# The last ten steps of a message-passing layer in another order: a closer bound on finished nodes, other blocks behind the last sums

## The chip, the cores and the metric

The kernel runs on one core of a Trainium2 chip. The metric is device time in microseconds for one execution. TensorE is called PE here, VectorE DVE, ScalarE ACT, GpSimd POOL and SyncE SP.

## The reference, cut to what matters

One graph layer over 12,500 nodes with 128 features and 400,000 edges that are sorted by destination, then a residual and a layer norm:

```python
rbf = exp(-(distances[:, None] - centers) ** 2 / (2 * width * width))      # 50 centers
cut = 0.5 * (cos(pi * distances / CUTOFF) + 1) * (distances <= CUTOFF)
W = (silu(rbf @ fw1 + fb1) @ fw2 + fb2) * cut[:, None]
messages = (h[src] @ pw + pb) * W
agg = segment_sum(messages, dst, num_segments=12500)
h_new = h + (silu(agg @ mw1 + mb1) @ mw2 + mb2)
out = layernorm(h + h_new)                                                 # h = x
```

Edges longer than the cutoff give nothing. With these inputs 71,145 of the 400,000 are kept. Destinations are drawn as 12,500 u² with u uniform, so the number of edges at or below node n grows with the root of n, and the node that the first p edges have reached grows with p².

## The kernel before, in words

**Edges.** The kept edges are packed to the front in seven chunks, in order of destination, and then worked on in *quads* of 512 edges: 139 steps, `q` = 0 to `NL` - 1 = 138. A quad is two *pairs* of 256 edges, and each pair has a base, the first destination it touches. Quads of the last three chunks (from 69 on) are summed in two windows, one a pair; a window is at most 128 nodes wide. For each quad POOL gathers 512 rows of the projected features from DRAM with four indirect DMAs (L1016; eight quads have one part that SP copies row by row instead). PE and ACT make the radial weights (`basis`, `first`, `silu`, `second`), and DVE multiplies the two (`message`, L1094), builds a matrix that puts each edge on its node (`place`, L1106: the hot matrix), and PE sums with it (`sum_up`, L1126). DVE adds a window of sums to `aggT`, the table of all nodes in SBUF (`add`, L1160), at a base that a register holds (`base_of` one at a time, `bases_of` several). `added(q)` says how many quads' sums are in the table before step q: in pairs early on, one quad late, from NL - 14, without delay from NL - 4.

**Nodes.** Since destinations are sorted, a node is finished once the sums have passed it. `done_to(p)` bounds from below the node that pair p begins at: 0.162 (p - 4.9)². The bound is checked on the chip: `limits` (L344) makes it per pair, `unpack` compares it with the true bases, `count` (L1320) adds what failed, and a number over zero starts a repair behind the main program (`tc.If`, L1612). Node blocks of four tiles of 128 nodes (0 to 76), and at the end those of `TAIL` (80 and 84 with four tiles, 88 with two, 90 with one, 91 with two, 93 with three, 96 with the last two, the very last of 84 rows), go through these steps: `load_x`, `node_first` (PE with `mw1`, ACT's silu, L1169 and L1171), `node_second` (PE with `mw2`, L328), `node_stats` (DVE adds 2x and takes statistics, L1187 and L1191), `deviations` (DVE, and ACT's root, L1198 to L1202), `scales` (DVE, L1209), `normalize` (ACT, or DVE for tiles named in `on`; then a store, L171). Blocks 0 to 76 have their steps in `begin`, from `done_to`; those of the tail are written out by hand in `nodes`, `tail` and the lines behind the loop (L1515 to L1538).

**What sets the order.** The program is scheduled by hand: each engine does its instructions in the order written, and waits for what it needs. One step of the loop (L1451) issues `message`, then `nodes`, the gathers of later quads, `second` for two quads ahead, fillers on PE (`keep_busy`: matmuls whose result is not used), `sum_up`, the base registers, `place` for the next quad, `add`, `tail`. ACT must load a table when it goes from Silu to Square and Exp or to Sqrt and back; `activation(warm, half_pi, AF.Silu)` loads one ahead of need. PSUM has four banks that are handed out in turn, x tiles eight buffers.

In the kernel before, the last two steps and the end run like this: step NL - 2 sends message 137, block 90's second node step, block 88's statistics, block 84's normalization, PE's sums of 137, then the message of quad 138 in parts of one gather each as far as the third, the adds of 137 and block 91's first node step. Behind the loop come the last part and its sums, block 91's second step, the adds of 138, and then 90, 91, 93 and 96: five tiles (93 to 97) go through all node steps behind the last sums.

Of the kernel before, what the change touches and what calls it, by code (L numbers as in the profile page):

```python
# [15 lines left out]
OP = mybir.AluOpType  # L16
# [12 lines left out]
QT = 4  # L29
# [46 lines left out]
DONE = (0.162, 4.9)  # L76
TAIL = {80: 4, 84: 4, 88: 2, 90: 1, 91: 2, 93: 3, 96: 2}
# [4 lines left out]
def kernel(  # L82
# [59 lines left out]
    def load_x(t0, n=None):  # L142
        t = x4_sb[loaded[0] % X_BUFS]
        loaded[0] += 1
        node_dma(t0, t, x, False, n)
        x_sb[t0] = t
# [196 lines left out]

    def limits(v):  # L344
        for c in range(NC_):
            v.tensor_scalar(lim[:, c:c + 1], part_f[:64], float(2 * QB[c] - DONE[1]), 0.0,
                                    op0=OP.add, op1=OP.max)
        root = keep.tile([64, NC_], F32, name="root")
        v.tensor_scalar(root, lim, DONE[0], None, op0=OP.mult)
        v.tensor_mul(lim, root, lim)  # L350

    def done_to(p):
        return int(DONE[0] * max(p - DONE[1], 0) ** 2) - 1
# [798 lines left out]
    def added(q):  # L1152

        return max((q - 2) // 2 * 2 if q < NL - 14 else q - 1 if q < NL - 4 else q, 0)

    def add(q, ks=(0, 1)):
        pa = pa_of[q]
        for k in ks[:windows(q)]:
            to = aggT[:, ds(bases.pop((q, k)), wide(q))]
            nc.vector.tensor_add(to, to, pa[:, k * W:k * W + wide(q)])  # L1160

    zs_of, py_of, st_of = {}, {}, {}

    def node_first(t0):

        n = sum(rows(t0))
        pz = bank()
# [48 lines left out]
    def normalize(t0, rs, by, on=(), eng=nc.sync):  # L1216

        y = x_sb.pop(t0)
        for k, m in enumerate(rows(t0)):
            if k in on:  # L1220
                nc.vector.tensor_scalar(y[:m, k, :], y[:m, k, :], rs[:m, k:k + 1], by[:m, k:k + 1],
                                        op0=OP.mult, op1=OP.add)
            else:
                nc.scalar.activation(y[:m, k, :], y[:m, k, :], AF.Identity, bias=by[:m, k:k + 1],
                                     scale=rs[:m, k:k + 1])
        node_dma(t0, y, out, True, eng=eng)

# [29 lines left out]
    def nodes(q):  # L1257

        if deep:
            scales(*deep.pop())  # L1260
# [15 lines left out]
        for k, t0 in enumerate(TAIL):  # L1276
            if q == NL - 8 + k:
                load_x(t0)
        if q == NL - 5:
            st_of[0] = statistics()  # L1280
            node_stats(80, st_of[0])
        if q == NL - 3:
            node_stats(84, st_of[0][:, 4:])
            dev_of.append(deviations([84], st_of[0][:, 4:]))
            nc.scalar.activation(warm, half_pi, AF.Silu)
        if q == NL - 2:
            node_second(90)
            st_of[1] = statistics()
            node_stats(88, st_of[1])
            scales(*dev_of.pop(0))  # L1290
            normalize(*ready.pop(0))

    st_of, deep, dev_of = {}, [], []

    def tail(q):

        if q == NL - 7:
            node_first(80)
        if q == NL - 6:
            node_second(80)  # L1300
        if q == NL - 5:
            keep_busy(8)
            node_first(84)
        if q == NL - 4:
            node_second(84)
            node_first(88)
        if q == NL - 3:
            node_second(88)
            node_first(90)
        if q == NL - 2:  # L1310
            node_first(91)
# [8 lines left out]
    def count():  # L1320
# [8 lines left out]
        nc.vector.tensor_reduce(miss[:, 2:3], late_f, AX.X, OP.min)  # L1329
        nc.vector.tensor_scalar(miss[:, 2:3], miss[:, 2:3], 0.0, None, op0=OP.is_lt)  # L1330
        nc.vector.tensor_reduce(miss[:, 3:4], low, AX.X, OP.min)
        nc.vector.tensor_scalar(miss[:, 3:4], miss[:, 3:4], -2 * CUTOFF, None, op0=OP.is_lt)
        cp = bank()
        nc.tensor.matmul(cp[:1, :5], ones[:, 0:1], miss[:, :5], start=True, stop=True)
        nc.vector.tensor_reduce(miss[0:1, 0:1], cp[:1, :4], AX.X, OP.add)
        nc.vector.tensor_scalar(miss[0:1, 1:2], cp[:1, 4:5], float(-NL * QE), 0.0,
                                op0=OP.add, op1=OP.max)
        nc.vector.tensor_add(miss[0:1, 2:3], miss[0:1, 0:1], miss[0:1, 1:2])
# [112 lines left out]
    for q in range(NL - 1):  # L1451
# [29 lines left out]
        if at_once:  # L1481
            bases_of(list(now))
        else:
            for k in now:
                base_of(k, (0,))
        if q < NL - 2:
            place(q + 1)
        if q == NL - 4:
            place(NL - 1)
        if q == NL - 2:  # L1490
            for j in range(QT - 1):
                sum_up(NL - 1, message(NL - 1, (j, j + 1)), (j,))
        for k in now:
            if not at_once:
                base_of(k, (1,))
            if q == NL - 5 and k == now[0]:
                deep.append(deviations([80], st_of[0]))
                nc.scalar.activation(warm, half_pi, AF.Silu)
# [16 lines left out]
    q = NL - 1  # L1515
    base_of(q)
    sum_up(q, message(q, (QT - 1, QT)), (QT - 1,))
    node_second(91)
    add(q)
    node_stats(90, st_of[1][:, 2:])  # L1520
    for t0 in (93, 96):
        node_first(t0)
    node_stats(91, st_of[1][:, 3:])
    early_dev = deviations([88, 90, 91], st_of[1])
    assert not ready
    for t0 in (93, 96):
        node_second(t0)
    st = statistics()
    node_stats(93, st)
    scales(*early_dev)  # L1530
    for _ in (88, 90):
        normalize(*ready.pop(0))
    node_stats(96, st[:, 3:])
    last_dev = deviations([93, 96], st)
    normalize(*ready.pop(0), on=(0,))
# [111 lines left out]
```

## Time and profile before

| what | us |
|---|---|
| three runs, median (lowest, highest) | 726.54 (725.65, 727.59) |
| the profiled execution | 726.45 |
| its span, first to last instruction | 724.6 |
| busy in the span: PE, DVE, POOL, ACT | 586.3, 560.9, 532.7, 403.9 |
| first gather of the last quad starts | 700.59 |
| end of the last gather on POOL | 705.27 |
| last store issued | 719.76 |

The profile is of one execution. A row of its timeline gives the start from the span's first instruction, the duration, the engine, the line, the operation with output and inputs, and in brackets how long the engine had been idle and what ended it. PE's granted clock is given as a share of full speed; its mean is 0.912. DMA issue, register loads and branches are not counted as busy.

### The profile page before, as it was taken

To read this page: it belongs to the slowest core of one execution; us is meant where nothing else is said; L and a number is where in the kernel's file an instruction comes from. 1 tells how busy PE (TensorE), PEld (TensorE's weight loads), DVE (VectorE), ACT (ScalarE), POOL (GpSimd) and SP (SyncE) were. 2 spreads that over 40 slices of the span, in tenths; PEclk is the share of its full clock that TensorE was granted. 3 is DMA by queue.
4 is the path that set the end of the run, shared out by engine and by line. 5 is a ranking of instruction groups with operands and counts; after the bars stand their busy time and mean duration, and the time that the engine had idled before them with its cause. 6 is when DMAs were issued, how large, how long until landed. Compare 5 with 4: busy or idle time off the path is not lost.

```text
span 724.6 us, 13518 instructions
## 1 busy us (share of the span) xinstructions
PE 586.3 (81%) x3531; PEld 463.4 (64%) x3531; DVE 560.9 (77%) x1734; ACT 403.9 (56%) x573; POOL 532.7 (74%) x569
## 2 busy tenths in 40 slices
PE   6778868698889787598758896999896788797874
PEld 6666557676667566477536684877674566575753
DVE  8899799689999898699969794967556455564774
ACT  7547625364556566275444467557645744374683
POOL 6777777777777777777777777777777777777770
PEclk9998788899999899699988999899899988999996
DMA  8995442443334332433334344534443433345251
GB/s 278 324 314 182 146 125 75 112 115 96 100 90 127 98 94 74 147 93 89 98 102 113 100 125 121 158 98 138 115 112 98 141 98 109 102 122 149 57 154 56
DMA packets 53104, 91.38 MB, mean 126 GB/s; under 512 B 13824, under 2 KB 20576, under 8 KB 53018
## 3 DMA queue, kind: packets, MB, share of 16 engines
q1 hardware_dynamic: 34610, 53.34, 22.2%
q0 software_dynamic: 17840, 36.77, 20.5%
q8 instruction: 30, 0.49, 0.3%
q14 instruction: 56, 0.46, 0.2%
q10 hardware_dynamic: 568, 0.33, 0.2%
HBM read 74.59 MB, written 15.79 MB: 125 GB/s over the span
## 4 chain that ended last, share of the span: by engine, by line
DVE 29%; PE 19%; POOL 16%; DMA 14%; issue 14%; ACT 5%; DVEq 2%; SPq 1%; ACTq 0%; POOLq 0%
POOL quad L1016 14%; DMA quad<-proj,srci 8%; DVE hot L1106 6%; PE ph L1066 4%; PE bank L1083 4%; DVE msg L1094 3%; PE sums L1126 3%; PE bank L328 3%; POOL x L1016 2%; DVE aggT L1160 2%; DVE bank L492 2%; DVE nodes L496 2%; DVE r_d L486 2%; DMA x<-proj,srci 1%; DVEq L1135 1%
## 5 line engine op out<-in xcount | busy, mean ns | idle before, releaser
L1016 POOL DMA_INDIRECT quad<-proj,srci x405 | 384.5, 949 | 123.5 <-issue 98.8
L1083 PEld LDWEIGHTS bank<-fw_sb,s 128*128 128x128 f32 x1112 | 159.2, 206 | 61.5 <-issue 51.2
L1072 ACT ACTIVATE s<-ph 128x1024 f32<-128x1024 f32 x70 | 71.3, 1018 | 160.7 <-PE ph L1066 160.6
L1083 PE MATMUL bank<-fw_sb,s 128*128 128x128 f32 x1112 | 159.3, 290 | 0.0
L1066 PE MATMUL ph<-rbf,w_sb 102*128 102x512 f32 x278 | 138.8, 623 | 10.6 <-ACT s L1072 6.5
L1126 PEld LDWEIGHTS sums<-hot,msg 128*128 128x128 f32 x816 | 110.0, 201 | 50.1 <-issue 25.3
L1126 PE MATMUL sums<-hot,msg 128*128 128x80 f32 (+4 forms) x816 | 112.9, 284 | 10.5 <-DVE msg L1094 10.2
L1106 DVE TENSOR_SCALAR hot<-iota_n,dl,cut 128x80 f32<-128x80 f32 (+4 forms) x408 | 108.8, 339 | 14.7 <-PE sums L1126 12.9
L1016 POOL DMA_INDIRECT x<-proj,srci x95 | 90.8, 956 | 29.0 <-issue 24.1
L1080 PE MATMUL bank<-fb_b,ones_b 96*128 96x512 bf16 x139 | 56.1, 404 | 42.7 <-DVE msg L1094 15.6
L1094 DVE TENSOR_TENSOR msg<-bank,quad 128x512 f32<-128x512 f32 (+1 forms) x78 | 52.8, 677 | 43.0 <-DMA quad<-proj,srci 32.3
L1066 PEld LDWEIGHTS ph<-rbf,w_sb 102*128 102x128 f32 x278 | 49.2, 197 | 46.9 <-issue 35.2
L1160 DVE TENSOR_TENSOR aggT<-aggT,sums 128x80 f32 (+4 forms) x209 | 53.9, 258 | 28.0 <-PE sums L1126 11.9
L1057 ACT ACTIVATE rbf<-d,rbf_bias,rbf_scale 102x512 f32<-102x512 f32 x70 | 56.2, 803 | 33.3 <-DMA d<-near_d 33.3
L1016 POOL DMA_INDIRECT quad<-in_x_dram,srci x48 | 47.3, 985 | 15.4 <-issue 12.5
L328 PEld LDWEIGHTS bank<-pw_sb,xT 128*128 128x128 f32 (+1 forms) x292 | 41.6, 206 | 10.8 <-issue 5.5
L1094 DVE TENSOR_TENSOR quad<-bank,quad 128x512 f32<-128x512 f32 (+2 forms) x40 | 25.2, 633 | 28.2 <-DMA quad<-proj,srci 23.7
L1072 ACT ACT_TABLE_LOAD x36 | 46.2, 1283 | 0.6
L1126 PE MATMUL sums<-quad,quad 128*128 128x128 f32 (+3 forms) x296 | 44.9, 302 | 1.6 <-DVE quad L1094 1.5
L1058 ACT ACT_TABLE_LOAD x35 | 44.9, 1283 | 0.6
L1058 ACT ACTIVATE rbf<-rbf 102x512 f32<-102x512 f32 x70 | 44.1, 630 | 1.5
L1126 PEld LDWEIGHTS sums<-quad,quad 128*128 128x128 f32 x296 | 42.5, 220 | 2.4 <-DVE quad L1094 2.2
(268 smaller groups left out, 816.6 us busy)
## 6 DMA issues: line engine op xcount, KB each, us to landing
d<-near_d SPq DMA_DIRECT2D x70, 256.0 KB
dl<-proj SPq DMA_DIRECT2D x1024, 0.5 KB
x<-in_x_dram SPq DMA_DIRECT2D x46, 256.0 KB
quad<-proj,srci POOLq DMA_INDIRECT x405
proj<-hp SPq DMA_DIRECT2D x24, 256.0 KB
out_dram<-x SPq DMA_DIRECT2D x22, 256.0 KB
x<-proj,srci POOLq DMA_INDIRECT x95
r_d<-in_edge_weight_dram SPq DMA_DIRECT2D x5, 256.0 KB
```

The lines of the kernel that those rows point to most:

```text
L328: nc.tensor.matmul(to[:m, k, :], lT[:, k * P:k * P + m], w, start=False, stop=(k == a + c - 1))
L1016: nc.gpsimd.indirect_dma_start(out=got[:, j, :], out_offset=None, in_=proj if table is None else table, in_offset=bass.IndirectOffsetOnAxi ...
L1057: nc.scalar.activation(rbf[:u], d[:u], AF.Square, bias=rbf_bias[:u], scale=rbf_scale[:u])
L1058: nc.scalar.activation(rbf[:u], rbf[:u], AF.Exp, scale=-1.0 / (2.0 * width * width))
L1066: nc.tensor.matmul(ph[:, h, :], w1_sb[:2 * KR, h, :], rbf[:2 * KR], start=True, stop=True)
L1072: nc.scalar.activation(s[:, :n], ph[:, :n], AF.Silu)
L1080: nc.tensor.matmul(pu, ones_b[:, :P], bias_b["fb2"].rearrange("k j f -> k (j f)"), start=True, stop=False)
L1083: nc.tensor.matmul(pu[:, j * H:(j + 1) * H], s[:, j * P:(j + 1) * P], fw2_sb, start=False, stop=(j == QT - 1))
L1094: nc.vector.tensor_mul(msg[:, a:b, :], pu_of[q].rearrange("p (j f) -> p j f", j=QT)[:, a:b, :], got_of[q][:, a:b, :])
L1106: nc.vector.tensor_scalar(hot[:, j, :wide(q)], iota_n[:, :wide(q)], dl[:, at[0], at[1]], cut[:, at[0], at[1]], op0=OP.is_equal, op1=OP.mult)
L1126: nc.tensor.matmul(pa[:, k * W:k * W + wide(q)], msg[:, j, :], hot[:, j, :wide(q)], start=(j % n == 0), stop=(j % n == n - 1))
L1160: nc.vector.tensor_add(to, to, pa[:, k * W:k * W + wide(q)])
```

## The change

It reorders the steps from NL - 12 on and the lines behind the loop.

- **Bound.** `DONE` takes a smaller shift (2.0 for chunks 0 to 3, 1.3 for 4 to 6, instead of 4.9), and `LAST` raises it to four fixed nodes at pairs 268, 270, 274 and 276. The test in `limits` follows.
- **Branch.** A base under the bound no longer counts into the part of the repair that computes everything anew but into the one that goes over the nodes again, which now covers all blocks.
- **Blocks.** The tail is 80, 84 (four tiles), 88, 90, 92, 94, 96 (two each). Sums go in without delay from NL - 8 (before: NL - 4). Block 80 begins at NL - 9 (NL - 7), 84 at NL - 7 (NL - 5), 88 at NL - 6 (NL - 4), 90 at NL - 5 (NL - 3), 92 at NL - 3, and 94 and 96 behind the loop. The same formula gives blocks 40 and 52 to 76 a step earlier, 68 two.
- **Loads.** The tail's x tiles are loaded at NL - 12, - 11, - 10, - 9, - 5, - 5 and - 4 (before: one a step from NL - 8).
- **End.** The loop ends one step earlier; steps NL - 2 and NL - 1 are written out. Quad 138 goes in four parts, the first window added before the last part. Blocks 92 and 94 do their node steps between these parts; 96 is the only block whose first node step waits for the last sums. A Sqrt table load stands before the last two roots. The bases of quads 136 to 138 are loaded at once at NL - 3, and the hot matrix of 138 in that step (before: NL - 4).

The core of the diff:

```diff
-DONE = (0.162, 4.9)
-TAIL = {80: 4, 84: 4, 88: 2, 90: 1, 91: 2, 93: 3, 96: 2}
+DONE = (0.162, 2.0, 1.3)
+LAST = {268: 11520, 270: 11776, 274: 12032, 276: 12288}
+TAIL = {80: 4, 84: 4, 88: 2, 90: 2, 92: 2, 94: 2, 96: 2}
+LOAD_AT = {80: 12, 84: 11, 88: 10, 90: 9, 92: 5, 94: 5, 96: 4}
...
     def limits(v):
...
+        for p, n in LAST.items():
+            v.tensor_scalar(root[:, 0:1], part_f[:64], p - 2 * QB[-2] - 0.5, float(n),
+                            op0=OP.is_gt, op1=OP.mult)
+            v.tensor_tensor(lim[:, NC_ - 1:], lim[:, NC_ - 1:], root[:, 0:1], OP.max)
     def done_to(p):
-        return int(DONE[0] * max(p - DONE[1], 0) ** 2) - 1
+        s = shift_of(chunk_of(p // 2)) if p < 2 * NQ else 0
+        return max([int(DONE[0] * max(p - s, 0) ** 2) - 1] + [n for k, n in LAST.items() if p >= k])
...
-        return max((q - 2) // 2 * 2 if q < NL - 14 else q - 1 if q < NL - 4 else q, 0)
+        return max((q - 2) // 2 * 2 if q < NL - 14 else q - 1 if q < NL - 8 else q, 0)
...
     def nodes(q):
-        if deep:
-            scales(*deep.pop())
+        while deep:
+            scales(*deep.pop(0))
...
-        for k, t0 in enumerate(TAIL):
-            if q == NL - 8 + k:
+        for t0, k in LOAD_AT.items():
+            if q == NL - k:
                 load_x(t0)
...
+        for k, group, t0, at in ((6, [], 80, 0), (5, [80, 84], 84, 4), (4, [], 88, 0), (3, [88, 90], 90, 2)):
+            if q == NL - k:
+                if at == 0:
+                    st_of[1] = statistics()
+                node_stats(t0, st_of[1][:, at:])
+                if group:
+                    deep.append(deviations(group, st_of[1]))
+                    nc.scalar.activation(warm, half_pi, AF.Silu)
...
     def tail(q):
...
+        for k, t0, step in ((9, 80, node_first), (8, 80, node_second), (7, 84, node_first),
+                            (6, 84, node_second), (6, 88, node_first), (5, 88, node_second),
+                            (5, 90, node_first), (4, 90, node_second), (3, 92, node_first)):
+            if q == NL - k:
+                step(t0)
+        if NL - 6 < q < NL - 2:
+            keep_busy(4)
...
-    for q in range(NL - 1):
+    for q in range(NL - 2):
...
+        elif q == NL - 3:
+            bases_of([q, q + 1, q + 2])
...
+        for k in {NL - 4: (q + 1, q + 2), NL - 3: (q + 2,)}.get(q, (q + 1,)):
+            place(k)
...
+    p, q = NL - 2, NL - 1
+    msg = message(p)
+    scales(*deep.pop(0))
+    while ready:
+        normalize(*ready.pop(0))
+    node_second(92)
+    keep_busy(6)
+    sum_up(p, msg)
+    st = statistics()
+    node_stats(92, st)
+    sum_up(q, message(q, (0, 1)), (0,))
+    dev = deviations([92], st)
+    nc.scalar.activation(warm, half_pi, AF.Silu)
+    sum_up(q, message(q, (1, 2)), (1,))
+    add(p)
+    node_first(94)
+    scales(*dev)
+    sum_up(q, message(q, (2, 3)), (2,))
+    add(q, (0,))
+    keep_busy(2)
+    for _ in range(len(ready)):
+        normalize(*ready.pop(0))
+    sum_up(q, message(q, (3, 4)), (3,))
+    node_second(94)
+    add(q, (1,))
+    node_first(96)
+    nc.scalar.activation(warm, half_pi, AF.Sqrt)
+    node_stats(94, st[:, 2:])
+    keep_busy(2)
+    node_second(96)
+    devs = [deviations([94], st[:, 2:])]
+    node_stats(96, st[:, 4:])
+    devs.append(deviations([96], st[:, 4:]))
+    for dev in devs:
+        scales(*dev)
...
+    for t0, k in ((94, 0), (96, 0), (96, 1), (94, 1)):
+        scaled(*ys[t0], k, (t0, k) in ((96, 0), (94, 1)))
+    for a, eng in ((0, nc.sync), (1, nc.scalar)):
+        m = rows(96)[a]
+        eng.dma_start(out[(96 + a) * P:(96 + a) * P + m], ys[96][1][:m, a])
+    node_dma(94, ys[94][1], out, True)
```

`scaled` is the normalization of one tile, taken out of `normalize`. The lines that these replace (L1276 to L1291, L1297 to L1311, L1486 to L1498, L1515 to L1538) are in the listing above.

106 lines of the change are left out of this document (29 added, 77 removed).

## The prediction

> **What bounds the kernel now.** I read the page, then the windows by stage, then the timeline of the last 50 us. Times are us from the span's start. Steps are named by their quad, 0 to 138: NL-7 is step 132, NL-1 is 138. "Block 92" is the block of node tiles that begins at tile 92.
>
> ```profile
> L1016 POOL DMA_INDIRECT quad<-proj,srci x405 | 384.5, 949 | 123.5 <-issue 98.8
> ...
> L1072 ACT ACTIVATE s<-ph 128x1024 f32<-128x1024 f32 x70 | 71.3, 1018 | 160.7 <-PE ph L1066 160.6
> ```
> ```profile
> 600.00:640.00 40.00, 32.84 (x176) 25.06 (x176) 22.89 (x78) 19.17 (x25) 30.23 (x33) 0.87 0.36 105
> ...
> 690.00:700.00 10.00, 7.69 (x37) 5.20 (x36) 7.18 (x27) 8.40 (x18) 7.56 (x9) 0.83 0.49 151
> ...
> 706.00:710.00 4.00, 4.00 (x19) 3.79 (x18) 1.24 (x5) 1.04 (x3) 0.00 (x0) 0.57 0.23 82
> ...
> 718.50:724.60 6.10, 0.00 (x0) 0.00 (x0) 0.00 (x0) 0.00 (x0) 0.00 (x0) 0.50 0.24 76
> ```
>
> The columns of the windows are busy us (and instructions) of PE, PEld, DVE, ACT and POOL, then PE's granted clock; those of the timeline below are start, duration, engine, line, operation, and the idle time before it. In the first fence a gather costs POOL 0.95 us, and the idle time before the gathers (123.5 us over 405) is mostly issue, 0.25 us each. The row 600:640 has 33 gathers in 40 us: about 1.25 us for one, 5.0 us for a quad of four, and nothing between. PE and DVE are far from full there (32.8 and 22.9 of 40 us). **POOL's gathers set the pace**, and the change leaves their number and order alone. So only what follows the last gather can give time, and what the new order puts late before it can cost some.
>
> ```profile
> 678.26 0.69 DVE L1094 TENSOR_TENSOR msg<-bank,quad 128x512 f32<-128x512 f32 x1 [0.72 <-DMA quad<-proj,srci]
> ...
> 684.35 1.05 PE L1126 MATMUL sums<-hot,msg 128*128 128x128 f32 x8
> ...
> 688.11 3.19 ACT L1224 ACTIVATE x<-x,by,rs 128x128 f32<-128x128 f32 x8 [0.73 <-DVE by L1210]
> ...
> 692.76 2.08 PE L1169 MATMUL bank<-aggT,mw_sb 128*128 128x512 f32 x2 [1.90 <-DVE aggT L1160]
> ...
> 693.22 0.17 DVE L1209 RECIPROCAL rs<-dev 128x4 f32<-128x4 f32 x1
> 693.42 0.16 DVE L1210 SCALAR_TENSOR_TENSOR by<-both_m,rs 128x4 f32<-128x4 f32 x1
> ...
> 699.62 0.38 ACT L1171 ACTIVATE zs<-bank 128x256 f32<-128x256 f32 x1 [1.09 <-PE bank L1169]
> ...
> 701.94 1.11 DVE L1106 TENSOR_SCALAR hot<-iota_n,dl,cut 128x128 f32<-128x128 f32 x4 [0.26 <-issue]
> 702.18 1.28 ACT L1202 ACT_TABLE_LOAD   x1
> ...
> 703.47 0.30 ACT L1202 ACTIVATE dev<-v,eps 128x4 f32<-128x4 f32 x1
> 703.49 0.68 DVE L1094 TENSOR_TENSOR msg<-bank,quad 128x512 f32<-128x512 f32 x1
> ...
> 704.20 0.36 DVE L1187 SCALAR_TENSOR_TENSOR x<-x,bank 128x256 f32<-128x256 f32 x1
> 704.33 0.94 POOL L1016 DMA_INDIRECT quad<-proj,srci  x1 [0.30 <-issue]
> 704.59 0.49 DVE L1191 BATCH_NORM_STATS2 st<-x 128x6 f32<-128x128 f32 x2
> ...
> 705.08 0.20 ACT L1285 ACTIVATE warm<-half_pi 128x1 f32<-128x1 f32 x1
> ...
> 705.39 1.65 ACT L1224 ACTIVATE x<-x,by,rs 128x128 f32<-128x128 f32 x4
> 705.50 0.22 PE L325 MATMUL bank<-mb_b,ones_b 96*128 96x128 bf16 x1 [1.38 <-ACT zs L1171]
> ```
> ```profile
> 706.26 1.86 PE L1126 MATMUL sums<-hot,msg 128*128 128x128 f32 x8
> 706.61 0.29 DVE L1094 TENSOR_TENSOR quad<-bank,quad 128x128 f32<-128x128 f32 x1 [0.53 <-DMA quad<-proj,srci]
> ...
> 708.16 0.61 DVE L1160 TENSOR_TENSOR aggT<-aggT,sums 128x128 f32 x2 [1.26 <-PE sums L1126]
> ...
> 709.27 0.29 DVE L1094 TENSOR_TENSOR quad<-bank,quad 128x128 f32<-128x128 f32 x1 [0.50 <-issue]
> ...
> 710.01 0.39 PE L1126 MATMUL sums<-quad,quad 128*128 128x128 f32 x2
> ...
> 710.43 0.61 DVE L1160 TENSOR_TENSOR aggT<-aggT,sums 128x128 f32 x2 [0.86 <-PE sums L1126]
> ...
> 712.16 0.54 PE L1169 MATMUL bank<-aggT,mw_sb 128*128 128x212 f32 x2
> ...
> 712.44 0.17 DVE L1198 TENSOR_TENSOR dif<-st 128x5 f32<-128x5 f32 x1
> ...
> 712.84 0.17 DVE L1201 TENSOR_TENSOR v<-both_m,dif 128x5 f32<-128x5 f32 x1
> ...
> 714.03 0.40 PE L328 MATMUL bank<-mw_sb,zs 128*84 128x128 f32 x2
> ...
> 715.34 0.48 DVE L1187 SCALAR_TENSOR_TENSOR x<-x,bank 128x128 f32<-128x128 f32 x2
> ...
> 715.74 0.47 DVE L1191 BATCH_NORM_STATS2 st<-x 128x6 f32<-128x128 f32 x2
> ...
> 716.74 0.34 DVE L1221 TENSOR_SCALAR x<-x,rs,by 128x128 f32<-128x128 f32 x1
> ...
> 718.50 1.26 ACTq L171 DMA_DIRECT2D out_dram<-x  x2
> ```
>
> The last gather starts at 704.33 and ends at 705.27; the span ends 19.3 us later. The third part of quad 138 (its gather started 703.08, one period of 1.25 before the last) was waited for until 706.61, about 3.5 us after its start, so the last part is there by some 707.8 at the latest. Its message, however, starts at 709.27: DVE stood at 708.16 for PE's sums of quad 137, and PE stood at 705.50 for ACT, which had done a load of the Sqrt table, one of the Silu table (702.18 to 705.28) and block 90's silu. So 1.5 us lie between the data and the message. Then come 10.5 us to the last store's issue (718.50 + 1.26 = 719.76) with five tiles in them (93 to 97), and 4.84 us (719.76 to 724.6) in which no engine computes: stores land, programs end.
>
> **The change part by part.**
>
> *The bound and its test.* `limits` gets eight more instructions on a 64x1 column, chained in pairs, and `count` one.
>
> ```profile
> 74.54 0.16 DVE L350 TENSOR_TENSOR lim<-root,lim 64x7 f32<-64x7 f32 x1
> 75.82 0.41 DVE L936 SCALAR_TENSOR_TENSOR dl<-dl 10x256 f32<-10x256 f32 x1 [1.12 <-ACT dl L927]
> ```
>
> The nearest row is the product at 74.54: 0.16 us, 0.19 if each waits for the one before, so at most 1.5 us. DVE idles 1.12 us right behind, for ACT, and that covers them but for 0.4 us; POOL's queue was filled before. I take 0, keep 0 to 0.4, and see no way to a gain. The bound must hold for these inputs, or the repair at the end runs. Counted in the inputs: 71,145 edges are kept, room is 71,168; the pair with least room is pair 27 (destination 107, bound 101.25), and of the four fixed ones pair 270 (11,790 against 11,776). It holds everywhere.
>
> *Early blocks.* With the closer bound, blocks 40 and 52 to 76 begin one step earlier (68 two), and 80 begins at NL-9 instead of NL-7.
>
> ```profile
> 653.93 0.69 DVE L1094 TENSOR_TENSOR quad<-bank,quad 128x512 f32<-128x512 f32 x1 [3.11 <-DMA quad<-proj,srci]
> ```
>
> DVE has such waits for the gather (3.11 us here) in these steps; they hide one more pair of adds or 0.87 us of statistics. Cost 0, while a step's work stays under 5.0 us; without that cover, the work itself.
>
> *Steps 132 to 137*, counted forward from message 132 with the rows' durations, each engine in its program's order. A step's DVE work: message 0.6, statistics 1.6 for four tiles or 0.8 for two (704.20 to 705.0), deviations 0.6 (712.44 to 713.01), scales 0.4, hot matrix 1.1, both adds 0.55; for base registers, which leave no busy row, I take 0.3 (above 0, and at most the 0.50 us of issue ahead of the message at 709.27, in which quad 138's are loaded). Message 132 at 678.26, then 4.75 us of work: message 133 at 683.0. It comes in two parts: 5.1 us with scales and four-tile statistics, message 134 at 688.0. Another 4.7: message 135 at 692.7. These are the gathers' own times within a us.
>
> ACT is the tight queue: a block of four tiles costs it 3.2 us to normalize (688.11), a Sqrt 1.28 + 0.3, the Silu after it 1.28 + 0.2. Step 132's Sqrt waits for DVE until 681.1; Silu load to 682.7, silu of quads 136 and 137 to 683.7, block 84's to 684.8 (its sums come 1.1 us behind the adds at 683.1), blocks 64 and 68 to 688.0, silu of quad 138 and of block 88 to 689.4, blocks 72 and 76 to 692.6, Sqrt to 694.2, Silu to 695.7, block 90 to 696.1, blocks 80 and 84 to 699.3, Sqrt to 700.9, Silu to 702.4. So in step 135 DVE waits at `scales` until 694.2, 0.9 us behind its message, and behind it stand block 88's statistics, two hot matrices and the adds (0.8 + 0.4 + 2.2 + 0.3 + 0.55): message 136 at 698.4, step 136 (0.6 + 0.8 + 0.6 + 0.4 + 1.1 + 0.55) to 702.5. **Message 137 at 702.5** instead of 703.49, where its gathers have just landed.
>
> PE per step: the adds' wait, node work, two matmul groups of 1.1 and 0.9 (684.35: eight matmuls), the fillers: 3.7 to 4.7 us at full clock, under 5.0.
>
> *The loads of x* move up: 80 to 90 to steps 127 to 130, where their buffers' last stores are two steps old; 92 and 94 stand on SP's queue behind the stores of 72 and 76 (692.6), 96 behind those of 80 and 84 (699.3). Block 92 is needed at 704.3, 96 at 711: cost 0 unless ACT slips some 8 us.
>
> *The end.* After message 137: scales, block 92's statistics behind PE's node step (704.3 to 705.1), part 0 of quad 138. PE: node step to 704.3, six fillers to 705.6, sums 137 to 706.5. ACT: blocks 88 and 90 in 1.65 to 705.3, Sqrt load and deviation to 706.9, Silu to 708.4, block 94's silu to 708.8. DVE: adds 137 to 707.1, then scales of 92 (ACT at 706.9) to 707.5, part 2 there, add of the first window, **last part at 708.2** instead of 709.27: gain 1.1. It is still not the gather's time, because two messages stand behind `scales`.
>
> From there: message and sums 1.2 (709.27 to 710.40), to 709.4; PE's second step for block 94 to 709.9; first step for 96, whose add is done, 0.6 with its bias: 710.5; silu 0.4: 711.0; second step 0.8, two tiles like the one at 714.03: 711.8; two sums with x and two statistics 0.87: 712.7; deviations 0.6: 713.3; ACT's root 0.3 with the table loaded beforehand; two scales 0.8 beside and behind it: 714.1; a normalization of a tile each on ACT (1.65 for four) and DVE, two deep: 714.6; issue 0.6: 715.2 on ACT, about the same on SP. That is 7.0 us where 10.5 were, gain 3.5. SP's last store is now 128 KB and its queue ends as late as ACT's, for which I take back 0.3. **Sum: 1.1 + 3.5 - 0.3 = 4.3 us.** The profiled execution took 726.45 us, of which 1.85 lie around the span; its time is 0.09 under the median of 726.54. So 726.45 - 4.3 = 722.2 us.
>
> *A rule against it.* PE's clock fell after short gaps: 1.90 us at 692.76, whose pair took 2.08 us (the window has 0.83), 1.38 us at 705.50 (0.57; eight matmuls in 1.86 instead of 1.05). The new order has one such gap in step 132, while PE waits for the adds behind block 76's statistics (sums done near 680.8, adds from 682.6: 1.8 us), and only shorter ones behind the fillers. The Trainium skill, "TensorE: Matmul & The Clock Gate", Part 1, drops the clock only after an idle window of about 3.4 us; by it no gap here would lower the clock and the sum would stand. The rows disagree, so the drop is a rival.
>
> **The rivals.**
>
> *ACT ends late* (chance 0.20): each 1 us that ACT's chain lies behind my count moves `scales` in step 135 and all behind it, since message 137 has no slack left. For it: nine table loads in its queue and little idle; against it: every term is a row. Two us late gives 724.2.
>
> *Half clock at the end* (0.08): the PE pieces between 708.5 and 711.8 are 2.9 us at full clock; doubled, as at 706.26, they take 2.9 more: 725.1.
>
> *Half clock from step 132 on* (0.09), the other side: the adds of a step now wait for that step's sums from NL-8 on, and node steps wait for the adds, so PE and DVE run in one loop. At full clock a round is under 4.7 us; at half clock PE's 3.5 us become 7 and the round 7.5 to 8. From 5.0 us on the loop, not the gathers, sets the pace: 2.5 us or more in each of three or four steps, 8 to 10 us, against the 4.3 gained: 730. For it: the gap in step 132 and the window of 0.57; against it: fillers in steps 134 to 137, and the clock came back within 10 us each time.
>
> *The bound fails and the repair runs* (0.01): some 27 blocks one after another, each of several us: over 800. The count of the inputs speaks against it.
>
> *Table loads with a drain* (0.01): the deviation at 703.47 starts 0.01 us behind the end of its 1.28 us load. If a switch held ACT as long again as its load, nine of them from step 132 on would add 11.5 us: 733. A hold of that kind is the rule of the Trainium skill, "ScalarE: Activation LUTs", What ACT_TABLE_LOAD costs (2.66 us for every switch, load and drain); the row at 703.47 contradicts it.
>
> **How the numbers follow.** The forecast, 722.2, has 0.61; its own range is 720.6 (last part at 707.0, soon after it lands, and 0.4 less behind it) to 723.8. With ACT's 724.2 to 724.6 and the clock's 725.1 the range to 725.5 holds eight in ten. 0.3% is 2.2 us, about what a measurement of this kernel can tell from no change: faster by more, below 724.4, is the forecast and half of ACT's rival, 0.71; within, the other half and the short clock drop, 0.18; slower, the loop and the two small ones, 0.11.
>
> **What would show it.** The last gather again at 704 within 0.5 us (else the pace moved). Message 137 near 702.5; `scales` of step 135 waiting for ACT about 1 us; the last part's message near 708.2; from it to the last store's issue 7 us; one silu and one root behind the last sums. Wrong if PE's clock in 700 to 712 is under 0.8, if ACT's silu of block 94 comes after 710, or if messages 134 to 136 come over 1 us later than in the quoted rows.

## The result, and the profile after

The changed kernel took 1006.75 us (median of 6 runs, 1005.79 to 1007.4), the one before 725.96 beside it: a ratio of 1.3866 (1.3846 to 1.3885). The forecast was 722.2. Three rows of the page of the changed kernel, whose span is 1005.5 us, say where to look: POOL's busy tenths in 40 slices, PE's clock in the same slices, and the group of the gathers (count, busy us and mean ns, idle us before them).

```profile
POOL 6777777777777777777777777777210000000000
...
PEclk9998778999889997997999989999866666655655
...
L1027 POOL DMA_INDIRECT quad<-proj,srci x413 | 392.3, 950 | 149.2 <-issue 98.2
```

A slice is 25 us. The program's own gathers end in slice 29, at 706.7 us, about where they ended before (705.27); slice 30 still has four gathers, and then follow ten slices without POOL, at a PE clock of 5 to 6 tenths. And there are 413 gathers, where 405 were: two quads of four more than the program's 139 steps need. That is code which stands in a branch behind the main program. Of the same page, the chain that ended last, by engine and by line:

```profile
ACT 12%; DVE 6%; PE 5%; issue 2%; DMA 0%; ACTq 0%; DVEq 0%
PE bank L331 5%; ACT x L1243 4%; ACT L1184 3%; DVE st L1204 2%; ACT L1215 2%; DVE x L1200 2%; ACT zs L1184 2%; ACT dev L1215 1%; DVE rs L1222 1%; DVE by L1223 0%; DVE v L1214 0%; DVE dif L1211 0%; DVE dif L1213 0%; DMA quad<-proj,srci 0%; PE sums L1137 0%
```

Nearly all of it is node work. The timeline shows one block of it:

```profile
770.40 1.65 ACT L1243 ACTIVATE x<-x,by,rs 128x128 f32<-128x128 f32 x4 [0.44 <-DVE by L1223]
772.06 1.28 ACT L1184 ACT_TABLE_LOAD   x1
...
773.35 0.60 ACT L1184 ACTIVATE zs<-bank 128x512 f32<-128x512 f32 x1
774.00 2.08 PE L331 MATMUL bank<-mw_sb,zs 128*128 128x128 f32 x8 [5.38 <-ACT zs L1184]
...
778.38 1.28 ACT L1215 ACT_TABLE_LOAD   x1 [4.43 <-DVE v L1214]
779.68 0.30 ACT L1215 ACTIVATE dev<-v,eps 128x4 f32<-128x4 f32 x1
...
780.42 1.65 ACT L1243 ACTIVATE x<-x,by,rs 128x128 f32<-128x128 f32 x4 [0.44 <-DVE by L1223]
```

One block of four tiles from 770.40 to 780.42, 10.0 us, each engine waiting for the one ahead of it, with two table loads on the way. **The repair ran**, the part of it that goes over the nodes again, now over all 27 blocks.

*Which pair fails.* Chunk 0 is read as 128 rows of edges, and the first 32 kept edges of each row go to quads 0 to 7. So the rest of chunk 0, up to quad 13, is not the sorted list's continuation: it goes over the rows again, from the first one on, with what remained of each. Quad 13 has base 91. The new bound for its two pairs, 26 and 27, which the test of chunk 1 covers with the shift of 2.0, is 93.31 and 101.25; the old one was 72 and 79. No node block begins that early, so the alarm saves nothing.

The main program ends in front of the repair, and its windows can be held against those of before (columns as in the prediction):

```profile
600.00:640.00 40.00, 31.06 (x179) 23.06 (x178) 22.30 (x74) 22.27 (x33) 30.24 (x33) 0.96 0.40 113
690.00:700.00 10.00, 7.45 (x49) 6.00 (x48) 8.44 (x33) 8.72 (x20) 7.56 (x9) 0.93 0.54 162
706.00:710.00 4.00, 2.38 (x16) 1.48 (x15) 2.56 (x10) 3.94 (x8) 3.09 (x4) 1.00 0.22 61
```

33 gathers in 40 us again, so the pace is the same. In 706 to 710 PE now has its full clock (0.57 before), but it computes for 2.38 us of 4; ACT is full. The rows of step 135 show most of the reason, in the order of time:

```profile
694.86 0.69 DVE L1105 TENSOR_TENSOR quad<-bank,quad 128x512 f32<-128x512 f32 x1
694.87 1.28 ACT L1215 ACT_TABLE_LOAD   x1
...
696.49 1.28 ACT L1304 ACT_TABLE_LOAD   x1
696.50 0.20 DVE L1222 RECIPROCAL rs<-dev 128x8 f32<-128x8 f32 x1 [0.94 <-ACT dev L1215]
...
697.89 0.36 ACT L1184 ACTIVATE zs<-bank 128x256 f32<-128x256 f32 x1
...
698.30 0.38 PE L1091 MATMUL bank<-fb_b,ones_b 96*128 96x512 bf16 x1 [1.74 <-ACT zs L1184]
698.52 1.83 PE L1094 MATMUL bank<-fw_sb,s 128*128 128x128 f32 x8
...
700.99 1.55 PE L1137 MATMUL sums<-quad,quad 128*128 128x128 f32 x8
...
702.58 0.61 DVE L1171 TENSOR_TENSOR aggT<-aggT,sums 128x128 f32 x2 [2.71 <-PE sums L1137]
...
703.53 0.69 DVE L1105 TENSOR_TENSOR msg<-bank,quad 128x512 f32<-128x512 f32 x1 [0.34 <-DVE aggT L1171]
```

PE's `second` for quad 137 stands 1.74 us for ACT's silu of block 90 (697.89). It needs none of its data; the bank that is handed out next is the one this silu still has to read, and the silu stands behind two table loads. Then the eight matmuls take 1.83 us (1.06 at full clock), the sums come at 700.99, DVE waits 2.71 us for them, and message 136 starts at 703.53 instead of the forecast 698.4. Not all of these 5.1 us come from step 135: message 132, which waited for its gather, was 1.3 us late (679.54), and message 135 was 2.2 us late (694.86, forecast 692.7). Step 135 itself took 8.67 us from message to message, forecast 5.7, and so added 3.0.

```profile
705.72 0.95 POOL L1027 DMA_INDIRECT quad<-proj,srci  x1 [0.30 <-issue]
...
706.44 1.11 DVE L1117 TENSOR_SCALAR quad<-iota_n,dl,cut 128x128 f32<-128x128 f32 x4 [0.78 <-issue]
...
714.34 0.28 DVE L1105 TENSOR_TENSOR quad<-bank,quad 128x128 f32<-128x128 f32 x1
...
720.54 0.37 SPq L174 DMA_DIRECT2D out_dram<-x  x1
```

The last gather of quad 138 starts at 705.72 (those behind it are the repair's), 1.4 us later than before and outside the 704 within 0.5 that the forecast named as its sign; the base registers take 0.78 us of issue at 706.44. The last part's message is at 714.34, and the last store's issue ends at 720.91 (720.54 + 0.37). So two questions went to the chip: what the repair costs, and why the main program, which ought to have ended 4.3 us sooner, did not.

### The profile page after: what moved, and what is told of

The parts are those of the page before. It is cut to its first block, busy times and chain, and to the rows that moved or that the text cites. A ratio compares the mean times of both kernels' runs of the same rounds, so it can differ in the third digit from the quotient of the medians.

```text
span 1005.5 us, 14992 instructions
## 1 busy us (share of the span) xinstructions
PE 707.7 (70%) x3886; PEld 533.1 (53%) x3886; DVE 631.0 (63%) x2076; ACT 546.5 (54%) x794; POOL 540.6 (54%) x577
## 5 line engine op out<-in xcount | busy, mean ns | idle before, releaser
L1027 POOL DMA_INDIRECT quad<-proj,srci x413 | 392.3, 950 | 149.2 <-issue 98.2
L331 PE MATMUL bank<-mw_sb,zs 128*128 128x128 f32 x392 | 78.4, 359 | 143.7 <-ACT zs L1184 143.7
L1094 PE MATMUL bank<-fw_sb,s 128*128 128x128 f32 x1128 | 164.5, 293 | 0.5 <-ACT s L1083 0.5
L1083 ACT ACTIVATE s<-ph 128x1024 f32<-128x1024 f32 (+1 forms) x72 | 72.4, 1005 | 169.0 <-PE ph L1077 168.9
L331 PEld LDWEIGHTS bank<-mw_sb,zs 128*128 128x128 f32 x392 | 69.4, 259 | 173.1 <-ACT zs L1184 172.0
L1077 PE MATMUL ph<-rbf,w_sb 102*128 102x512 f32 x282 | 147.0, 646 | 18.6 <-ACT rbf L1069 16.1
L1200 DVE SCALAR_TENSOR_TENSOR x<-x,bank 128x512 f32<-128x512 f32 (+3 forms) x56 | 33.9, 609 | 143.8 <-PE bank L331 143.8
L1243 ACT ACTIVATE x<-x,by,rs 128x128 f32<-128x128 f32 x194 | 79.6, 482 | 14.3 <-DVE by L1223 14.3
L1182 PE MATMUL bank<-aggT,mw_sb 128*128 128x512 f32 (+2 forms) x108 | 71.1, 750 | 5.5 <-DVE aggT L1171 5.3
L1184 ACT ACTIVATE zs<-bank 128x512 f32<-128x512 f32 (+2 forms) x54 | 30.0, 555 | 42.6 <-PE bank L1182 42.2
```

The source lines that it names most:

```text
L331: nc.tensor.matmul(to[:m, k, :], lT[:, k * P:k * P + m], w, start=False, stop=(k == a + c - 1))
L1027: nc.gpsimd.indirect_dma_start(out=got[:, j, :], out_offset=None, in_=proj if table is None else table, in_offset=bass.IndirectOffsetOnAxi ...
L1077: nc.tensor.matmul(ph[:, h, :], w1_sb[:2 * KR, h, :], rbf[:2 * KR], start=True, stop=True)
L1083: nc.scalar.activation(s[:, :n], ph[:, :n], AF.Silu)
L1094: nc.tensor.matmul(pu[:, j * H:(j + 1) * H], s[:, j * P:(j + 1) * P], fw2_sb, start=False, stop=(j == QT - 1))
L1182: nc.tensor.matmul(pz[:, :n], mw1_sb, aggT[:, t0 * P:t0 * P + n], start=False, stop=True)
```

## The experiments

The first four ran on one chip (before: 727.28 us there).

**bound_ok.** The closer bound everywhere but in chunk 1's test:

```diff
-            v.tensor_scalar(lim[:, c:c + 1], part_f[:64], float(2 * QB[c] - shift_of(c)), 0.0,
+            v.tensor_scalar(lim[:, c:c + 1], part_f[:64], float(2 * QB[c] - (4.9 if c == 1 else shift_of(c))), 0.0,
```

> The changed kernel with one edit: the tested bound of chunk 1 has the old shift of 4.9. Theory A: the repair ran only because the first pairs of chunk 1 (26 and 27, base 91) lie under their new bounds of 93.3 and 101.3; then 405 gathers instead of 413, no repair, and by the trace of the changed kernel the main path ends with the last store's issue at 720.9, so the span ends near 725.7 and the time is near 727.5, no gain over the kernel before. Rival 1: another pair fails too, the repair stays and so do 1006 us. Rival 2: the main path in that trace is slowed by the repair's own gathers, and the recorded sum of 722.2 stands.

731.05 us, ratio 1.0045 (1.0031 to 1.0058). So chunk 1's pairs alone set off the repair, and it costs 1006.75 - 731.05 = 276 us. And the new order is slower than the old even without it. The 727.5 of theory A was too low by 3.5: in this profile the last gather starts 2.1 us later than in the changed kernel's, and the end behind the last store's issue takes 6.6 us instead of 4.84.

**few_blocks.** The changed kernel, with fewer blocks in the repair that runs:

```diff
             for q in range(NL, NQ):
                 more(q)
-            finish(blocks)
+            finish(list(TAIL))
```

> The changed kernel with its bound as it is, and a repair that goes over the 7 blocks of the tail instead of all 27 (the other nodes keep the main path's values). If the repair's cost is its blocks one by one, 10.0 us each as the rows between 760 and 800 show, it takes 20 of 10.0 less: about 806. If it were the two extra quads and their code, over 950.

808.05 us, in one run: 198.7 us less for 20 blocks, 9.9 each, as the 10.0 us between the rows at 770.40 and 780.42 say.

**bank_turn.** bound_ok, and in three steps `second` takes the bank behind the next one:

```diff
         s = s_of.pop(q)
+        if NL - 4 <= q < NL - 1:
+            free.append(free.pop(0))
         pu = bank()
```

> bound_ok, and second of quads 135, 136 and 137 takes the next PSUM bank in turn instead of the first, which block 90's (or 84's, 88's) first node step has just given back. Theory B: the main path lost its gain because PE stood 1.74 us for that bank until ACT's silu, behind two table loads, and the slow clock that followed: second of 137 starts right behind the fillers, message 136 comes 2 to 3 us earlier, the time is 2 to 4 us under bound_ok. Theory C: ACT's queue as a whole is late; then the same time as bound_ok within 1 us.

728.52 us, ratio 1.0019 (1.0003 to 1.0035), 2.5 under bound_ok. Its timeline:

```profile
696.02 0.38 PE L1093 MATMUL bank<-fb_b,ones_b 96*128 96x512 bf16 x1
...
697.56 1.05 PE L1139 MATMUL sums<-quad,quad 128*128 128x128 f32 x8
...
699.39 0.60 DVE L1173 TENSOR_TENSOR aggT<-aggT,sums 128x128 f32 x2
...
700.28 0.69 DVE L1107 TENSOR_TENSOR msg<-bank,quad 128x512 f32<-128x512 f32 x1 [0.28 <-DVE aggT L1173]
...
711.17 0.28 DVE L1107 TENSOR_TENSOR quad<-bank,quad 128x128 f32<-128x128 f32 x1
...
717.37 0.37 SPq L174 DMA_DIRECT2D out_dram<-x  x1
```

`second` no longer waits, the sums take 1.05 us instead of 1.55, DVE's adds follow without a wait, and message 136 is at 700.28. From message 135 (694.48) to it are 5.8 us, as forecast (5.7).

**root_later.** bound_ok, with the deviations of blocks 80 and 84 and the Silu load behind that step's node work instead of ahead of it:

```diff
-                if group:
+                if group and k != 5:
...
+        if q == NL - 5:
+            deep.append(deviations([80, 84], st_of[1]))
+            nc.scalar.activation(warm, half_pi, AF.Silu)
         if NL - 6 < q < NL - 2:
             keep_busy(4)
```

> bound_ok, and in step 134 the deviations of blocks 80 and 84 with their two table loads stand behind block 90's first node step, so its silu comes ahead of the loads. Theory B: second of 137 starts some 1.5 us earlier, but DVE waits up to 1 us longer at the scales of step 135: 0 to 2 us under bound_ok, less than bank_turn. Theory C: slower than bound_ok or the same.

731.16 us, ratio 1.0053 (1.0040 to 1.0067): no gain. But the wait for the bank is gone here too, and the profile shows where the gain went:

```profile
698.20 0.38 PE L1091 MATMUL bank<-fb_b,ones_b 96*128 96x512 bf16 x1
...
703.76 0.69 DVE L1105 TENSOR_TENSOR msg<-bank,quad 128x512 f32<-128x512 f32 x1 [0.29 <-DVE aggT L1171]
...
708.35 0.85 PE L1182 MATMUL bank<-aggT,mw_sb 128*128 128x256 f32 x2 [2.58 <-DVE aggT L1171]
...
709.00 1.91 PE L1325 MATMUL ph<-mb_b,ones_b 96*128 96x512 bf16 x4
...
712.02 0.42 DVE L1200 SCALAR_TENSOR_TENSOR x<-x,bank 128x256 f32<-128x256 f32 x1 [2.73 <-PE bank L331]
```

`second` starts at 698.20 without a wait, and message 136 comes 3.8 us ahead of the last gather's start, where it came 2.3 ahead in bound_ok: 1.5 us won, as theory B said. Then, in step 136, PE waits 2.58 us for the adds and goes on at half clock (0.56 granted from 708.3 to 712; four fillers take 1.91 us instead of 1.03), and DVE waits 2.73 us for it. So the silu behind the two table loads did hold the bank, and this run's unchanged time doesn't clear the loads.

**turn_short, before_long, sums_first, early_alone.** These four ran on another chip; their edits stand with the second runs below.

> The kernel of bank_turn, with the repair of nodes (which does not run) written for the seven blocks of the tail, as in the kernel before, instead of for all 27: less code behind the main program, nothing else. Theory A (the 6.7 us from the last store's issue to the span's end, against 4.84 before, hold a wait of SP for its instructions, and where it falls depends on how much code is jumped over): the end is back near 4.9 us, and the time falls from 728.5 to 726.7. Theory B (the end is longer because SP's last store is now 128 KB, or for another reason that lies in the order of the main program): the end stays at 6.6 to 6.8 us, and the time at 728.5.

> The kernel before, with the repair of nodes (which does not run) written for all 27 blocks as in the changed kernel: more code behind the main program, nothing else. Theory A (the end's length comes from the code that is jumped over): the end goes from 4.84 us to about 6.7, and the time from 727.3 to 729.1. Theory B (it comes from the new order's last stores): the end stays at 4.8 to 4.9 and the time at 727.3.

> turn_short, with two more edits in the last steps: no fillers before the sums of quad 137 (in bank_turn's trace six of them held PE from 706.9 to 708.4 while the message had been there since 705.5), and in step 136 the adds stand ahead of the hot matrix of 138 (there DVE began the adds at 704.29, 1.8 us after PE had ended the sums). Theory A (behind the last gather DVE and PE wait for one another, and each of the two stands on that chain): the last part's message comes some 1.9 us sooner behind the last gather (5.67 us in bank_turn, 3.8 here), and the time is 1.9 us under turn_short's: 724.8 if that one is at 726.7. Theory B (without the fillers PE's clock falls and the pieces behind the last sums take double): the last part's message comes sooner, but from it to the last issue it is 8 to 9 us instead of 6.6, and the time is that of turn_short.

> The kernel before with the closer bound alone (with the old one for chunk 1, as in bound_ok), so that blocks 40 and 52 to 76 begin a step earlier and the test of the bound is the longer one; the tail, its order and the end stay as before. Theory A (the earlier blocks and the test cost nothing, and the last gather's start varies from run to run by a us): 727.3, within 0.7 us. Theory B (bank_turn's last gather began 1.2 us later than before, and bound_ok's 3.5 us later, because of the earlier blocks or the test): 728.5 or more, with the last gather 1 us or more later than 704.3.

On that chip all took 1,098 to 1,102 us, the kernel before too (1097.66), with ratios 1.0011, 0.9966, 1.0015 and 0.9974, whose intervals all hold 1. They tell nothing of 2 us. All four were run again, on a third chip.

**turn_short_again.** bank_turn, with the repair, which does not run, as long as before the change (`-finish(blocks)`, `+finish(list(TAIL))`).

> The kernel of turn_short again, because on the chip of its first run every kernel, the one before too, took some 1,098 us, with waits for issue all over, which hides 2 us. Theory A (the end is longer in bank_turn because SP waits for its instructions, and that hangs on the code that is jumped over): from the last store's issue to the span's end about 4.9 us instead of 6.76, and a ratio to the kernel before near 0.9995 instead of 1.0019. Theory B (the end is longer for a reason in the main program's order): 6.6 to 6.8 us and 1.0019.

726.54 us, ratio 1.0002 (0.9986 to 1.0017). SP's instructions at the program's last line (count, ns, first and last start) in the kernel before, in bank_turn and in turn_short_again:

```profile
L1643 SPq EVENT_SEMAPHORE  x14: 17/28/28, 722.9 to 724.5; - x14
```
```profile
L1665 SPq EVENT_SEMAPHORE  x14: 17/28/28, 721.7 to 724.4; - x14
```
```profile
L1665 SPq EVENT_SEMAPHORE  x14: 17/28/28, 721.2 to 722.8; - x14
```

The same 14 semaphores take 1.6, 2.7 and 1.6 us. From the last issue to the span's end it is 4.84, 6.8 and 5.2 us. The semaphores and the end are shorter, as theory A said (5.2 us, where it said 4.9); the ratio's interval overlaps with bank_turn's, so the next run asks it of the kernel before.

**before_long_again.** The kernel before, with the opposite edit (`-finish(list(TAIL))`, `+finish(blocks)`): only code that is jumped over.

> The kernel of before_long again: the kernel before with more code behind the main program, that does not run. Theory A (the end's length comes from the code that is jumped over, through a fetch of instructions in the middle of SP's last semaphores): SP's 14 last semaphores take 2.7 to 2.9 us instead of 1.6, the span ends some 6.3 us after the last store's issue instead of 4.84, and the ratio to the kernel before is 1.0015 to 1.002. Theory B (it comes from the new order's last stores): 1.6 us, 4.8 to 4.9 us, ratio 1.000.

726.7 us against 725.57, ratio 1.0012 (1.0003 to 1.0021). SP's last semaphores, then the queue of instruction fetches (packets, MB, share) of this kernel and of the one before:

```profile
L1643 SPq EVENT_SEMAPHORE  x14: 17/28/28, 724.3 to 726.9; - x14
```
```profile
q14 instruction: 58, 0.48, 0.2%
```
```profile
q14 instruction: 56, 0.46, 0.2%
```

2.6 us instead of 1.6, and two more fetches; from the last issue to the span's end it is 6.2 us. These marks are theory A's. The ratio lies a little under its range, and says 0.9 us.

**early_alone_again.** The kernel before with the change's `DONE` and `LAST` and the lines of its diff in `limits` (chunk 1 as in bound_ok) and `done_to`:

```diff
-DONE = (0.162, 4.9)
+DONE = (0.162, 2.0, 1.3)
+LAST = {268: 11520, 270: 11776, 274: 12032, 276: 12288}
```

> The kernel of early_alone again: the kernel before with the closer bound alone (the old one for chunk 1), so blocks 40 and 52 to 76 a step earlier and the longer test. Theory A (they cost nothing): a ratio within 0.999 to 1.001. Theory B (they are what made the last gathers of bound_ok and bank_turn later): 1.0016 or more, and a last gather that begins 1.2 us or more behind the 704.33 of before.

Ratio 1.0017 (1.0003 to 1.0032): closer to theory B. The earlier blocks and the longer test cost some 1.2 us (0.2 to 2.3). The last gather starts at 706.21, 1.9 us later than in the profile of before. But that mark alone decides nothing: in before_long_again, whose main program is that of before, it starts at 707.71.

**sums_first_again.** turn_short, with two edits:

```diff
     node_second(92)
-    keep_busy(6)
     sum_up(p, msg)
...
+        if q == NL - 3:
+            add(q)
         for k in {NL - 4: (q + 1, q + 2), NL - 3: (q + 2,)}.get(q, (q + 1,)):
             place(k)
...
-            add(k)
+            if q < NL - 3:
+                add(k)
```

> The kernel of sums_first again, for the same reason. Theory A (behind the last gather DVE and PE wait for one another; the fillers ahead of the sums of 137 and the hot matrix ahead of the adds of 136 stand on that chain): the last part's message 3.8 us behind the start of the last gather instead of bank_turn's 5.67, and the time 1.9 us under that of turn_short_again. Theory B (without the fillers PE's clock falls): the message sooner, but 8 to 9 us instead of 6.6 from it to the last issue, and the time that of turn_short_again.

725.2 us, ratio 0.9971 (0.9956 to 0.9985): a little faster than the kernel before, but 1.3 us under turn_short_again, not 1.9; the last part's message comes 5.2 us behind the last gather, not 3.8. The clock did not fall (6.58 us from the last part's message to the last issue). Of the timeline, DVE's next waits:

```profile
710.00 0.17 DVE L1224 RECIPROCAL rs<-dev 128x2 f32<-128x2 f32 x1 [0.37 <-ACT dev L1217]
...
711.15 0.29 DVE L1173 TENSOR_TENSOR aggT<-aggT,sums 128x128 f32 x1 [0.58 <-PE sums L1139]
...
711.35 0.28 DVE L1107 TENSOR_TENSOR quad<-bank,quad 128x128 f32<-128x128 f32 x1
```

**parts_free.** sums_first, with the messages of quad 138 ahead of these two waits, the sums of 137 ahead of block 92's second step, and most fillers of the last three steps gone:

```diff
     msg = message(p)
+    sum_up(p, msg)
...
+    place(q)
     node_second(92)
-    sum_up(p, msg)
+    add(p)
...
     sum_up(q, message(q, (1, 2)), (1,))
-    add(p)
     node_first(94)
-    scales(*dev)
     sum_up(q, message(q, (2, 3)), (2,))
+    sum_up(q, message(q, (3, 4)), (3,))
     add(q, (0,))
-    keep_busy(2)
+    scales(*dev)
...
-    sum_up(q, message(q, (3, 4)), (3,))
     node_second(94)
```

> sums_first with the waits taken out that its trace still shows in the last two steps: the message of 137 ahead of the hot matrix of 138 and its sums ahead of block 92's second step (they began 0.95 us after the fourth filler could have ended), the last two messages ahead of the scales of block 92 (these waited 0.37 us for ACT) and of the first window's add (0.58 us for PE), no fillers in the last three steps. Theory A (the chain behind the last gather was DVE's and PE's): the last part's message starts 3.6 to 4.0 us behind the last gather's start instead of 5.20, from it to the last issue 6.6 us, the time 1.3 us under the 725.2 of sums_first_again, a ratio near 0.9955. Theory B (PE's clock falls without fillers): the message that early, but 8 to 9 us behind it, and 725.2 or more.

724.27 us, ratio 0.9975 (0.9963 to 0.9987): by the ratio no better than sums_first_again. Its timeline:

```profile
709.09 0.68 DVE L1107 TENSOR_TENSOR quad<-bank,quad 128x128 f32<-128x128 f32 x3
...
709.93 1.28 ACT L1533 ACT_TABLE_LOAD   x1
...
711.34 0.36 ACT L1186 ACTIVATE zs<-bank 128x256 f32<-128x256 f32 x1
...
711.76 0.71 PE L331 MATMUL bank<-mw_sb,zs 128*128 128x128 f32 x4 [0.74 <-ACT zs L1186]
```

The last of the three messages starts near 709.5 (709.09 + 0.68 - 0.28), 3.4 us behind the last gather's 706.06, a little sooner than theory A said. But behind it are 8.2 us, theory B's size without its cause: PE's granted clock is 1.00 from 706 on, and PE waits for block 94's silu, which stands behind ACT's Silu load. That silu starts 5.3 us behind the last gather's start, in sums_first_again 5.2 (711.39): what DVE and PE won ends there, and ACT has become the bound.

The marks of the profiles on one scale, us; in brackets the time since the mark to the left (the forecast's 5.1 are 4.84 and the 0.3 for SP's queue):

| kernel | last gather starts | last part's message | last store issued | span ends |
|---|---|---|---|---|
| before | 704.33 | 709.27 (4.9) | 719.76 (10.5) | 724.6 (4.8) |
| forecast | 704.33 | 708.2 (3.9) | 715.2 (7.0) | 720.3 (5.1) |
| changed | 705.72 | 714.34 (8.6) | 720.91 (6.6) | repair |
| bound_ok | 707.79 | 716.28 (8.5) | 722.86 (6.6) | 729.5 (6.6) |
| root_later | 707.56 | 716.24 (8.7) | 722.81 (6.6) | 729.5 (6.7) |
| bank_turn | 705.50 | 711.17 (5.7) | 717.74 (6.6) | 724.5 (6.8) |
| turn_short_again | 705.14 | 710.99 (5.9) | 717.56 (6.6) | 722.8 (5.2) |
| sums_first_again | 706.15 | 711.35 (5.2) | 717.93 (6.6) | 723.5 (5.6) |
| parts_free | 706.06 | 709.5 (3.4) | 717.66 (8.2) | 723.0 (5.3) |
| before_long_again | 707.71 | 710.84 (3.1) | 720.78 (9.9) | 727.0 (6.2) |
| early_alone_again | 706.21 | 709.72 (3.5) | 719.69 (10.0) | 724.9 (5.2) |

## Why the prediction was wrong

**The failed step** is "The bound must hold for these inputs ... It holds everywhere." It was worked out as if pairs followed the sorted order: pair 27 was given destination 107, against a bound of 101.25. Its base is 91, because chunk 0's rows give their first 32 edges to quads 0 to 7. The rival "the bound fails and the repair runs" had the mechanism, the 27 blocks and "over 800", at a chance of 0.01. The step's price is 276 us, all but 9 of the 284.5 by which the forecast missed. A count of the bases as the kernel packs them gives it.

**The 9 us that are left** (731.05 for bound_ok, 722.2 forecast), by the table. In bound_ok's profile the span is 9.2 us over the forecast: the last gather starts 3.5 later, the last part's message comes 4.6 later behind it, the stretch to the last issue is 0.4 shorter and the end 1.5 longer.

- *The last part's message*, forecast 3.9 us behind the last gather, came 8.5. The failed step is "PE per step ... 3.7 to 4.7 us at full clock, under 5.0": it counts PE's work and not its wait for a bank, nor the half clock behind that wait. Handing the bank out differently took 2.8 us of it away (5.7 in bank_turn), fillers and adds in another order 0.5 to 0.7 more (5.2 in sums_first_again). The base registers of the last three quads took 0.78 us in step 136, whose sum has no term for them.
- *From that message to the last issue*, forecast 7.0, measured 6.6, in six profiles (10.5 before). This step was right, but for a detail: one silu stands behind the last sums, and two roots, not one (block 94's at 718.00, 96's at 719.01).
- *The end* was taken as 4.84 us and 0.3 for SP's queue, and came to 6.6. Turn_short_again has 5.2: the code of the repair is worth some 1.5 us in the profiles, 0.9 by before_long_again's ratio. The 0.4 that 5.2 lies over 4.84 can't be put down to SP's queue: early_alone_again, with the old last stores, has 5.2 too.
- *Early blocks and test*, "Cost 0", cost about 1.2 us (ratio 1.0017). Which of the two, and by what wait, stays open, and so does the rest of the 3.5 us by which bound_ok's last gather is late.
- *The gain of 1.1 us ahead of the message* leaned on one profile, in which 1.5 us lay between the data and the message. before_long_again, with the same main program, has none:

```profile
707.68 1.05 PE L1126 MATMUL sums<-hot,msg 128*128 128x128 f32 x8
707.71 0.95 POOL L1016 DMA_INDIRECT quad<-proj,srci  x1 [0.31 <-issue]
...
710.84 0.29 DVE L1094 TENSOR_TENSOR quad<-bank,quad 128x128 f32<-128x128 f32 x1 [0.77 <-DMA quad<-proj,srci]
```

There the message waits for the gather and comes 3.1 us behind its start. One difference is the clock: the sums of quad 137 took 1.05 us for eight matmuls there, and 1.86 in the profile that the forecast was read from. The last gather was 3.4 us later, the last issue only 1.0, and what the new order can win depends on the run: 15.4 us from the last gather to the last issue in the one profile of before and 13.1 in this one, against 12.2 in bank_turn. With all that the runs took away, the new order gains 1.8 to 2.1 us (ratios 0.9975 and 0.9971) of the 4.3 of the sum.

Two of the forecast's own signs of being wrong came: messages 134 to 136 were 2.2 to 5.1 us late, and block 94's silu started at 713.88, behind 710. The third did not: PE's clock from 700 to 712 was 0.92.

The other rivals: *ACT ends late* came in another form. ACT's chain was on time (`scales` of step 135 waited 0.94 us, forecast 0.9), but PE stood behind it, through the bank. *Half clock from 132 on* was right in the drop (1.83 us for eight matmuls behind a gap of 1.74) and wrong in its length, one step. The rule of the Trainium skill, "TensorE: Matmul & The Clock Gate", Part 1, drops the clock only after some 3.4 us of idling; the row at 698.52, behind 1.74 us, contradicts it here. A short gap need not lower it either: behind 2.37 us at 704.95 in bank_turn the granted clock stayed at 1.00, behind 2.58 us in root_later it was 0.56. *Table loads with a drain*: in the repair's block the deviation starts 0.02 us behind its load (778.38 + 1.28, then 779.68), so none shows. (This rival's sum, 722.2 + 11.5, is 733.7, not 733.)

What stays open: why the last gather of one main program starts at 704.33 in one execution and at 707.71 in another, 3.4 us apart, where the change was to bring 4.3.

## What to carry to other kernels

A bound that is tested on the chip has to be tried on the positions that the kernel's own packing gives, pair by pair, not on the sorted input; and a test that stands for a wrong answer is dear where its repair is serial (10 us a block). When work is moved, ask of every buffer handed out in turn who reads it last and what stands ahead of that reader: here a wait of 1.74 us for a bank, which no data needed, and the half clock behind it cost 2.5 us (731.05 against 728.52). A slack read from one execution is a gain only if a second execution has it too.

## What the runs showed of the hardware

- Code that is never run has a price: 20 more blocks in a branch that is jumped over, 2 more instruction fetches (58 for 56), 1.0 us more in SP's last 14 semaphores, 1.0012 in time. That a fetch holds SP there is argued from the counts, not shown.
- On one chip the kernel before and the four others that ran there took some 1,098 us. In turn_short's profile there DVE, POOL and ACT are busy for 564, 531 and 407 us, as in turn_short_again's (562, 533 and 406); PE, at a mean clock of 0.766 instead of 0.918, for 682 instead of 586. The gathers have the usual mean and 330 us of idle time before them instead of 123.5:

```profile
L1027 POOL DMA_INDIRECT quad<-proj,srci x405 | 384.8, 950 | 330.3 <-issue 109.7
```

Why is open; it is why 2 us could not be told there.
